# Second attention of a convolution sequence: the first projection's products ordered by input half, and the second item's denominators issued behind their step's filler

## The chip, the cores and the metric

The kernel runs on one core of a Trainium2 chip, in one launch, in float32 throughout. The metric is the device time of one execution in microseconds (us); lower is better. Times given for a kernel are medians of several runs.

## The reference

The input x has 16 images of 256 channels and 32x32 positions (1024 positions each). Two layers are applied to every image on its own. Cut to what matters here:

```python
# layer 0: attention with 4 heads of 64, softmax over the keys, a projection and a residual
qkv = xs @ w_proj + b_proj ; attn = softmax(q k^T * 64**-0.5) ; x = attn v @ w_out + b_out + xs
# layer 1, first half: group norm, attention with 8 heads of 32, a projection and a residual
qkv = group_norm(x) @ qkv_w.T
attn = softmax(q k^T * 32**-0.5 + phys_bias)
x = x + (attn v) @ proj_w.T + proj_b
# layer 1, second half: group norm and a two-layer MLP with GELU and a residual
x = x + mlp_w2 gelu(mlp_w1 group_norm(x) + mlp_b1) + mlp_b2
```

The change lies in layer 1's attention, called the second attention below (keys and tiles ending in `_b` or `b_...`); layer 0's is the first (`_a`).

## The kernel before, in words

**Stages.** `first_pass` walks over the 16 images (batches 0 to 15). For each it runs the first attention of image b, then dense work (the MLP's hidden layer of image b-1 and the products q, k, v of both attentions), then the second attention of image b. Work that does not depend on the attention is placed inside the second attention's steps as *filler*: the MLP's second layer of image b-1 (`reduce`, tiles m, products numbered 1 to 7) and products of the next image (v_a). Batches 1 to 14 take one form (`by_fold`); batches 0 and 15 take another, in which denominators are made in another way.

**Items and steps of the second attention.** An image has 1024 queries (two halves t of 512) and 8 heads (two halves c of 4 heads). An item is one pair (t, c): item 0 is (0,0), item 1 is (0,1), items 2 and 3 are the second query half. Each item goes over the 1024 keys in four units of two key blocks. `attention_b` is a generator: step n issues the scores of unit n (`scores`, tiles s_b, L569), weighs the unit before it (`weigh`, tiles acc_b, L621), and issues the additions of the exponentials on VectorE (tiles es_b, L595). The exponentials are ScalarE's (e_b, L582). Items 0 to 3 have units 0-3, 4-7, 8-11, 12-15.

**The planner.** `run` drives the generator. After step n it calls `later.tick()`, which runs what has come due, and then the filler listed for that step (`fill[n]`). `later.after(k, f)` puts f off by k ticks. All engines execute their own instructions in the order issued, so a place in this list is a place in each queue.

**Denominators.** When item i's last unit is weighed, `fold` packs its 128x2048 sums (es_b) into two slots of a tile `packed` of four slots (item 0 and 2: slots 0 and 1; item 1 and 3: slots 2 and 3). It uses one DMA from SyncE's queue and an accumulating one from GpSimd's queue (L651, L652). Some ticks later `normalise_folded` runs:

1. 8 matmuls on TensorE reduce `packed` to den (128x128) in PSUM bank 1 (den_b, L661; the profile counts 16, two for each).
2. ScalarE copies den to SBUF (rd_b, L376), and SyncE's queue spreads it (sp_b, L381).
3. At the next tick VectorE takes the reciprocal (inv_b, L387).
4. SyncE's queue writes it to DRAM (row_b, four issues, L391) and broadcasts it back (rd_b<-row_b, four issues, L403).
5. Some ticks later VectorE multiplies the item's result by it (`scale`, L703).

PSUM bank 1 has a single buffer. The scores of each step write their second 512-column group to that bank too.

**The first projection.** When item 1 has been scaled, the projection of the first query half is due one tick later (`out_proj`, tiles j, L357): two output halves co, each the sum over two input halves kc, each in four column strips of 32, so 16 matmuls (32 in the profile). Input half kc=0 is item 0's result, kc=1 is item 1's. Inside the second attention the two output halves share one two-bank PSUM tile, and both are read out after all products (ScalarE, L747). The readout goes to a *home*: slots 2 and 3 of the packed tile, handed over in `spare["home"]`. The projection of the second half is issued later, inside the next image's first attention.

**Who else uses the home.** While it is set, products 6 and 7 of the MLP are copied by ScalarE (L1213) into slot `number - 4` of the packed tile, that is slots 2 and 3. VectorE adds them to x from there (L1234).

**The step of the change.** Item 1 is folded in step 8, and its denominators come due at the tick of step 10. The filler of step 10 is product 6 in two parts of 256 columns (m, two times 32 matmuls in the profile). So TensorE's order in step 10 before the change is: weighing, den_b of item 1, product 6, then step 11's scores.

Of the kernel before, what the change touches and what calls it, by code (L numbers as in the profile page):

```python
# [14 lines left out]
P = 128  # L15
# [244 lines left out]
def first_pass(ctx, tc, x, out, k):  # L260
    nc = tc.nc
    B, C, S = x.shape
    CC, SB, NT = C // P, S // P, S // TB
    HC = k["m1b"].shape[1]
    later = Later()
# [44 lines left out]
    def wide(name, n=None):  # L310
        if n is None:
            n = next(m for m in order if m not in kept)
        use(n)
        return ps_s.tile([P, 2, TB], F32, tag=f"s{n}", name=name)

    def bank(name, n):
        return ps_a.tile([P, TB], F32, tag=f"b{n}", name=name)
# [36 lines left out]
    def product(o, w, r, **flags):  # L354
        for c0 in range(0, P, cols[0]):
            sl = slice(c0, c0 + cols[0])
            nc.tensor.matmul(o[sl], w[:, sl], r, **flags)  # L357
# [12 lines left out]
    def weights_tile(name):  # L370
        return work.tile([P, 4, TB], F32, tag="e", name=name, bufs=4)

    spread_out, spare = {}, {}

    def denominators(key, den, d, full, waits, then, parts=1):
        nc.scalar.copy(d, den)  # L376
# [165 lines left out]
    def attention_b(b, qT, kT, v, project):  # L542
# [9 lines left out]
        res, sums, packs, parts, count = {}, {}, [], [], [0]  # L552
# [94 lines left out]
        def fold(i, r):  # L647
            if i == 0:
                packs.append(act.tile([P, 4, TB], F32, tag="res", name=f"packed_{key}"))
            packed = packs[0][:, i % 2 * 2 : i % 2 * 2 + 2]  # L650
            nc.sync.dma_start(packed, sums[i][:HALF])  # L651
            nc.gpsimd.dma_start(packed, sums[i][HALF:], accum_op=ALU.add)  # L652
            later.after(3 if i == 1 else 4, lambda: normalise_folded(i, r, packed))

        def normalise_folded(i, r, packed):
            c = items[i][1]
            q = TB // G
            den = bank(f"den_{key}_{i}", 1)[:, :q]
            for m in range(2):
                for n in range(G):  # L660
                    nc.tensor.matmul(  # L661
                        den[n * D : (n + 1) * D, :], k["folded"][:, c, m],
                        packed[:, m, n * q : (n + 1) * q], start=m == 0, stop=m == 1,
                    )
            if i == 1:
                spare["home"] = packs[0]
            full = work.tile([P, TB], F32, tag="full", name=f"rd_{key}_{i}", bufs=2)
            denominators(
                f"{key}_{i}", den, full[:, :q], full, (1, 2 if i < 2 else 4),
                lambda full: scale(i, r, False, full), G,  # L670
            )
# [29 lines left out]
        def scale(i, r, last, full):  # L701
            t, c = items[i]
            tc.keep_in_program_order(nc.vector.tensor_mul(r, r, full))  # L703
            if c == CC - 1:
                issue = project(t, res[t])
                if last and b + 1 < B:
                    handed.append(issue)
                else:
                    later.after(1, issue)
# [23 lines left out]
    def out_proj(key, w, src, bias, xs, t, stats, then):  # L733
        todo = list(range(CC))

        def issue(cos=range(CC), apart=False):
            home = None if apart else spare.pop("home", None)
            apart = apart or cols[0] == P
            if not apart:
                both = wide(f"{key}_{t}")  # L740
            ps = {}

            def leave(co):
                y = xs[:, co, t * TB : (t + 1) * TB]
                if home is not None:
                    held = home[:, 2 + co]
                    nc.scalar.activation(  # L747
                        held, ps[co], AF.Identity, bias=bias[:, co : co + 1]
                    )
                    later.after(1, lambda: add_up(co, y, held))  # L750
                    return
                else:
                    nc.vector.scalar_tensor_tensor(
                        y, ps[co], bias[:, co : co + 1], y, ALU.add, ALU.add
                    )
                nc.vector.bn_stats(stats[:, co, t, :], y)
                todo.remove(co)

            def add_up(co, y, held):
                with tc.issue_after(spread_out["es"].ins):  # L760
                    nc.vector.tensor_add(y, y, held)
                    nc.vector.bn_stats(stats[:, co, t, :], y)

            for co in cos:
                ps[co] = bank(f"{key}_{t}_{co}", co) if apart else both[:, co, :]
                for kc in range(CC):
                    product(
                        ps[co],
                        w[:, kc, co * P : (co + 1) * P],
                        src(kc),  # L770
                        start=(kc == 0),
                        stop=(kc == CC - 1),
                    )
                if apart:
                    leave(co)
            if not apart:
                for co in cos:
                    leave(co)
            if not todo and then:
                then()  # L780

        return issue
# [310 lines left out]
    def mlp(b, xb):  # L1093
# [93 lines left out]
        def reduce(number, right, outs, then, part=0, parts=1):  # L1187
            size = TB // parts
            at = slice(part * size, (part + 1) * size)
            ps = wide(f"m2_{b}_{number}_{part}")[:, 0, :size]  # L1190
            for i in range(n4):
                product(
                    ps, blocks[2][number - 1][:, i * P : (i + 1) * P], gs[(*right, i)][:, at],
                    start=(i == 0), stop=(i == n4 - 1),
                )
            bias, num, m = None, 1, None
            if len(outs) == 1:
                bias = k["m2b2"]

                num = 2 if b == B - 1 and number == 7 else 1  # L1200
            elif number in (2, 5):
                bias = k["m2b"]
            co = outs[0][0]
            if len(outs) == 2 or "home" in spare:

                if not lent:
                    lent.append(act.tile([P, 4, TB], F32, tag="v0", name=f"lent_{b}"))
                if len(outs) == 2:
                    m = lent[0][:, number % 4]
                else:  # L1210
                    m = spare["home"][:, number - 4]
                if bias is not None:
                    nc.scalar.activation(m[:, at], ps, AF.Identity, bias=bias[:, co : co + 1])  # L1213
                    bias = None
                else:
                    nc.scalar.copy(m[:, at], ps)
                if part < parts - 1:
                    return
                ps = m
            assert parts == 1 or m is not None  # L1220

            def add_up():
                for co, t, plus in outs:
                    missing[co, t] -= 1
                    n = TB // num
                    for u in range(num):
                        sl = slice(t * TB + u * n, t * TB + (u + 1) * n)
                        y, p = xb[:, co, sl], ps[:, u * n : (u + 1) * n]
                        if bias is not None:
                            nc.vector.scalar_tensor_tensor(  # L1230
                                y, p, bias[:, co : co + 1], y, ALU.add, ALU.add
                            )
                        else:
                            (nc.vector.tensor_add if plus else nc.vector.tensor_sub)(y, y, p)  # L1234
                        if not missing[co, t]:
                            nc.sync.dma_start(out[b, co * P : (co + 1) * P, sl], y)
                if then:
                    for i in range(n4) if b == B - 1 else (None,):
                        combine(*then, True, i)


            if len(outs) == 2 and b < B - 1:
                later.after(1, add_up)
            else:
                add_up()
# [7 lines left out]
    def run(stage, fill=None):  # L1253
        for n, _ in enumerate(stage):
            pieces = fill.get(n, ()) if fill else ()
            if n > last:
                run_pieces(pieces, False)
            later.tick()
            if n <= last:
                run_pieces(pieces, False)  # L1260

    def run_pieces(pieces, tick=True):
        for piece in pieces:
            piece()
            if tick:
                later.tick()
# [14 lines left out]
    ps, n = bank("bqk", 0), brow.shape[0]  # L1281
# [4 lines left out]
    start = first_qk[::2] + first_qk[1::2] + first_v  # L1286
# [441 lines left out]
```

## Time and profile before

| | |
|---|---|
| median of 3 runs | 3623.34 us (3620.74 to 3624.38) |
| the profiled execution's own time | 3623.73 us |
| its span | 3621.7 us, at a granted TensorE clock of 0.998 |
| TensorE matmul busy | 3588.2 us (99%), 35,565 matmuls |
| VectorE busy | 2781.4 us (77%) |
| ScalarE busy | 2283.7 us (63%) |
| GpSimd busy | 229.9 us (6%) |

The profile is of one execution. The times are those of whole executions, 2.0 us longer than the span in the profiled one. The page of the profile gives busy time by engine, a chain of work that ended last, and groups of instructions by line and tile. The trace behind it gives each instruction's start. Ends of matmuls are modelled, so idle time of TensorE that is shorter than the modelled tail of a matmul does not show as idle. It shows as a longer distance from one start to the next.

### The profile page before, as it was taken

How to read it: one execution, taken by the hardware profiler on the slowest of the kernel's cores; microseconds unless marked ns; L12 is line 12 of the kernel's file. 1: busy time of each engine (PE TensorE's matmuls, PEld its weight loads, DVE VectorE, ACT ScalarE, POOL GpSimd, SP SyncE). 2: the span in 40 equal slices, each digit the busy share in tenths (PEclk: the TensorE clock that was granted, in tenths of full speed). 3: DMA queues.
4: the chain of work that ended last, by engine and by line, in shares of the span. 5: the costliest groups of instructions: out<-in, count | busy, mean ns of one | idle time of the engine just before them, and what ended most of it. 6: DMA issues, size and time to landing. Idle time of an engine off the chain costs nothing.

```text
span 3621.7 us, 81706 instructions
## 1 busy us (share of the span) xinstructions
PE 3588.2 (99%) x35565; PEld 1471.2 (41%) x35565; DVE 2781.4 (77%) x3181; ACT 2283.7 (63%) x3197; POOL 229.9 (6%) x317
## 2 busy tenths in 40 slices
PE   9999999999999999999999999999999999999998
PEld 3434344443443434434344443434434444343433
DVE  5586887868878687876878878688786977868887
ACT  4565757657576674756758566575765757657572
POOL 4000100001000010000000001000010100001000
PEclk9999999999999999999999999999999999999999
DMA  3011221203112131221312213121121212213100
GB/s 129 10 49 39 58 76 37 78 28 68 68 37 75 37 83 45 44 68 39 81 45 52 66 33 81 45 55 63 38 76 45 55 62 48 72 39 65 59 23 23
DMA packets 81572, 198.30 MB, mean 55 GB/s; under 512 B 37974, under 2 KB 38742, under 8 KB 75062
## 3 DMA queue, kind: packets, MB, share of 16 engines
q1 hardware_dynamic: 71828, 164.39, 14.9%
q0 software_dynamic: 7632, 28.21, 5.1%
q8 instruction: 281, 4.60, 0.5%
q14 instruction: 85, 0.70, 0.1%
q10 hardware_dynamic: 1746, 0.40, 0.1%
HBM read 125.85 MB, written 22.27 MB: 41 GB/s over the span
## 4 chain that ended last, share of the span: by engine, by line
PE 81%; DVE 8%; issue 4%; DMA 3%; SPq 2%; ACT 1%; DVEq 0%; ACTq 0%; POOL 0%
PE s_a L428 12%; PE acc_a L451 12%; PE m L1105 10%; PE s_b L569 8%; PE acc_b L621 8%; PE m L357 7%; DVE es_b L595 4%; PE qk_b L1011 3%; PE qk_a L1011 3%; PE v_b L357 3%; PE o L357 3%; PE j L357 3%; PE v_a L357 2%; DMA rd_b<-row_b 2%; PE qk7y_b L1011 1%
## 5 line engine op out<-in xcount | busy, mean ns | idle before, releaser
L582 ACT ACTIVATE e_b<-s_b 128x1024 f32<-128x1024 f32 (+1 forms) x1280 | 982.0, 865 | 137.1 <-PE s_b L569 137.1
L595 DVE TENSOR_TENSOR es_b<-es_b,e_b 128x2048 f32<-128x2048 f32 (+1 forms) x460 | 881.7, 1935 | 101.9 <-ACT e_b L582 85.9
L438 ACT ACTIVATE e_a<-s_a 128x1024 f32<-128x1024 f32 x512 | 520.8, 1024 | 360.2 <-PE s_a L428 357.4
L428 PE MATMUL s_a<-q,k 64*64 64x512 f32 x4096 | 544.3, 593 | 0.0
L451 PE MATMUL acc_a<-e_a,v 64*64 64x512 f32 x4096 | 540.2, 589 | 0.0
L569 PE MATMUL s_b<-q,k 32*64 32x512 f32 x8192 | 527.4, 600 | 4.0 <-DVE res_b L639 2.0
L465 DVE TENSOR_TENSOR es_a<-es_a,e_a 128x1024 f32<-128x1024 f32 x384 | 474.1, 1235 | 69.2 <-ACT e_a L438 49.7
L621 PE MATMUL acc_b<-e_b,v 128*32 128x512 f32 x4096 | 492.1, 598 | 0.0
L357 PE MATMUL m<-g,w 128*32 128x256 f32 (+1 forms) x6456 | 416.6, 385 | 0.0
L357 PEld LDWEIGHTS m<-g,w 128*32 128x32 f32 x6456 | 223.9, 111 | 204.3 <-issue 58.9
L451 PEld LDWEIGHTS acc_a<-e_a,v 64*64 64x64 f32 x4096 | 188.0, 133 | 251.5 <-issue 215.1
L569 PEld LDWEIGHTS s_b<-q,k 32*64 32x64 f32 x8192 | 175.8, 130 | 257.5 <-issue 132.6
L428 PEld LDWEIGHTS s_a<-q,k 64*64 64x64 f32 x4096 | 175.9, 133 | 246.7 <-issue 209.5
L621 PEld LDWEIGHTS acc_b<-e_b,v 128*32 128x32 f32 x4096 | 108.4, 109 | 351.6 <-ACT e_b L582 194.7
L1105 PE MATMUL m<-gn_h,w 128*128 128x512 f32 x512 | 242.3, 601 | 2.9 <-DVE x L1230 1.3
L595 DVE TENSOR_TENSOR es_b<-e_b,e_b 128x2048 f32<-128x2048 f32 (+1 forms) x72 | 147.0, 2051 | 127.8 <-ACT e_b L582 127.8
L1169 DVE TENSOR_TENSOR g<-g,g 128x512 f32<-128x512 f32 (+1 forms) x185 | 195.7, 1069 | 1.2 <-PE m L357 0.8
L1105 PE MATMUL m<-hs,w 128*128 128x512 f32 x384 | 177.9, 592 | 0.1
L1120 ACT ACTIVATE g<-g,m1b 128x512 f32<-128x512 f32 x128 | 91.7, 720 | 110.9 <-DVE g L1149 83.3
L1105 PEld LDWEIGHTS m<-gn_h,w 128*128 128x128 f32 x512 | 93.2, 190 | 118.6 <-issue 100.5
L1120 ACT ACTIVATE g<-m,m1b 128x512 f32<-128x512 f32 x128 | 80.9, 683 | 76.6 <-PE m L1105 76.6
L357 PE MATMUL v_a<-wp,x 128*32 128x256 f32 (+1 forms) x1856 | 121.5, 379 | 0.0
(215 smaller groups left out, 3537.5 us busy)
## 6 DMA issues: line engine op xcount, KB each, us to landing
w<-w_kept SPq DMA_DIRECT2D x30, 1792.0 KB
packed_b<-es_b SPq DMA_DIRECT2D x42, 512.0 KB
packed_b<-es_b POOLq DMA_DIRECT2D x42, 512.0 KB, 6.2
d_a<-row_a SPq DMA_DIRECT2D x64, 256.0 KB
rd_b<-row_b SPq DMA_DIRECT2D x252, 64.0 KB
out_dram<-x SPq DMA_DIRECT2D x63, 256.0 KB
x<-in_x_dram SPq DMA_DIRECT2D x30, 512.0 KB
qk<-qk_kept SPq DMA_DIRECT2D x14, 1024.0 KB
```

The lines of the kernel that those rows point to most:

```text
L357: nc.tensor.matmul(o[sl], w[:, sl], r, **flags)
L428: nc.tensor.matmul(s[h : h + HALF, g, :], kT[g * D : (g + 1) * D, c, kb * P + h : kb * P + h + HALF], qT[g * D : (g + 1) * D, c, t * TB : ...
L438: nc.scalar.activation(e, s, AF.Exp, scale=float(D) ** -0.5)
L451: nc.tensor.matmul(accs[i][h][g * D : (g + 1) * D, :], v[h * HALF : (h + 1) * HALF, kb, c * 2 + g], e[h * HALF : (h + 1) * HALF, g, :], st ...
L465: nc.vector.tensor_add(sums[i], held[i] if kb == 1 else sums[i], e)
L569: nc.tensor.matmul(outs[g][h : h + HALF, :], kT[g * D : (g + 1) * D, c, k0 : k0 + HALF], qT[g * D : (g + 1) * D, c, t * TB : (t + 1) * TB] ...
L582: nc.scalar.activation(to, s, AF.Exp, scale=float(D) ** -0.5)
L595: ins = nc.vector.tensor_add(d, (d if kb else es[0][:, g : g + step]), es[m][:, g : g + step])
L621: nc.tensor.matmul(acc[g * D : (g + 1) * D, :], v[:, kb + m, c * G + g], es[m][:, g, :], start=(m == 0), stop=(m == 1),)
L1011: nc.tensor.matmul(to, w, x[right], start=first, stop=True, skip_group_check=not first)
L1105: nc.tensor.matmul(ps, blocks[1][number - 1][:, i * P : (i + 1) * P], inputs[b][number], start=first, stop=True, skip_group_check=not first,)
L1169: (nc.vector.tensor_add if plus else nc.vector.tensor_sub)(d, d, more)
```

## The change

There are two edits to the order of issue, and one of a buffer that goes with the second.

1. In `out_proj`, where the two output halves share a tile, all products of input half 0 are issued first (both output halves), then all of input half 1. Before, output half 0 was finished before output half 1 was begun. Where the halves have banks of their own the order stays.
2. The denominators of item 1 (batches 1 to 14) are put on a list `behind` when they come due, and `run` issues them after the step's filler instead of ahead of it. The tick on which the rest depends stays the same.
3. Product 6 goes to slot 0 of the packed tile in place of slot 2 (`number % 6 * 3`; product 7 keeps slot 3), and `spare["home"]` is set when item 1 is folded.

```diff
-    spread_out, spare = {}, {}
+    spread_out, spare, behind = {}, {}, []
...
-            later.after(3 if i == 1 else 4, lambda: normalise_folded(i, r, packed))
+            if i == 1:
+                spare["home"] = packs[0]
+                later.after(3, lambda: behind.append(lambda: normalise_folded(i, r, packed)))
+            else:
+                later.after(4, lambda: normalise_folded(i, r, packed))
...
-            if i == 1:
-                spare["home"] = packs[0]
...
+            def part(co, kc):
+                product(
+                    ps[co],
+                    w[:, kc, co * P : (co + 1) * P],
+                    src(kc),
+                    start=(kc == 0),
+                    stop=(kc == CC - 1),
+                )
+
             for co in cos:
                 ps[co] = bank(f"{key}_{t}_{co}", co) if apart else both[:, co, :]
+            if apart:
+                for co in cos:
+                    for kc in range(CC):
+                        part(co, kc)
+                    leave(co)
+            else:
                 for kc in range(CC):
-                    product(
-                        ps[co],
-                        w[:, kc, co * P : (co + 1) * P],
-                        src(kc),
-                        start=(kc == 0),
-                        stop=(kc == CC - 1),
-                    )
-                if apart:
-                    leave(co)
-            if not apart:
+                    for co in cos:
+                        part(co, kc)
                 for co in cos:
                     leave(co)
...
-                    m = spare["home"][:, number - 4]
+                    m = spare["home"][:, number % 6 * 3]
...
             if n <= last:
                 run_pieces(pieces, False)
+            while behind:
+                behind.pop(0)()
```

No instruction is added or removed. On VectorE's, GpSimd's and SyncE's queues none changes its place. On TensorE's and ScalarE's queues the denominators of item 1 (8 matmuls and one copy) move behind product 6 (32 matmuls and two copies) in 14 batches, and the projection's products change order in all 16.

## Prediction

> **What bounds the kernel now.** I read the page first, then the waits of the projection's tile j, then the timeline at the two places that the change touches. Of the page, busy times and the chain that ended last:
>
> ```profile
> PE 3588.2 (99%) x35565; PEld 1471.2 (41%) x35565; DVE 2781.4 (77%) x3181; ACT 2283.7 (63%) x3197; POOL 229.9 (6%) x317
> ...
> PE 81%; DVE 8%; issue 4%; DMA 3%; SPq 2%; ACT 1%; DVEq 0%; ACTq 0%; POOL 0%
> ```
>
> TensorE sets the time almost everywhere. As no matmul is added or removed, the change can only shift stalls. The chain leaves TensorE once in each second attention and comes back at the projection. Timeline of TensorE there, batch 1 (start, length, engine, line, tiles, count, idle before and what ended it):
>
> ```profile
> 428.31 1.04 PE L357 MATMUL j<-res_b,wpj 128*32 128x512 f32 x8
> 430.72 2.78 PE L357 MATMUL j<-res_b,wpj 128*32 128x512 f32 x24 [1.37 <-DVE res_b L703]
> ```
>
> The 8 matmuls are output half 0 with input half 0. Then TensorE waits for VectorE's scaling of item 1. Undisturbed, a group of four 512-column matmuls starts every 0.42 us; here 1.96 us pass, so the stall is S = 1.54. The timeline gives the same distance for batches 1 to 14: 1.96, 1.07, 1.62, 1.15, 1.11, 0.94, 0.90, 0.51, 2.20, 1.06, 1.17, 0.94, 1.30, 0.50. Less 0.42 each, the stalls sum to 10.6 us. In batches 0 and 15 the projection has no such gap. So 10.6 us, 0.29% of the time, is all that edit 1 can touch.
>
> What makes the scaling late is not TensorE. The reciprocal of item 1 starts at 417.18 and the scaling at 429.97; between them lie SyncE's four row issues, the write, four broadcast issues and their landing. From item 0's scaling to item 1's reciprocal VectorE has no gap, and the distance is 6.39 to 6.43 us in every batch in which I read it, also in three in which TensorE had just lost a microsecond. VectorE and the transfers run on their own clock here, and TensorE waits for it.
>
> The second place, step 10 of batch 1:
>
> ```profile
> 402.48 0.62 PE L661 MATMUL den_b<-packed_b,folded 128*32 128x128 f32 x16
> 402.91 3.64 PE L357 MATMUL m<-g,w 128*32 128x256 f32 x64
> 404.10 0.34 ACT L376 COPY rd_b<-den_b 128x128 f32<-128x128 f32 x1
> 406.12 0.61 SPq L381 DMA_DIRECT2D sp_b<-rd_b  x1
> 406.48 1.97 PE L569 MATMUL s_b<-q,k 32*64 32x512 f32 x32
> 406.62 0.47 ACT L1213 ACTIVATE packed_b<-m,m2b 128x256 f32<-128x256 f32 x1 [1.20 <-PE m L357]
> ```
>
> Denominators, filler, next scores. ScalarE has emptied PSUM bank 1 at 404.44, two microseconds before the scores need it. In batches 2, 8 and 14 the denominators' packed transfer is late (batch 2):
>
> ```profile
> 624.73 1.47 PE L621 MATMUL acc_b<-e_b,v 128*32 128x512 f32 x12
> 627.00 0.64 PE L661 MATMUL den_b<-packed_b,folded 128*32 128x128 f32 x16 [0.81 <-DMA packed_b<-es_b]
> ```
>
> From the last weighing group to den_b it is 0.43 us in 11 batches, and 1.42, 1.35 and 1.41 in these three: stalls of 0.99, 0.92 and 0.98.
>
> **The Trainium skill.** "PSUM — Partial Sum Buffer", section "Engine vs sequencer instructions": ScalarE and VectorE work strictly first in, first out, and matmuls start and complete in program order. The trace agrees: TensorE stood 1.37 us at j with ready scores behind it. The same page, "PSUM bank collisions raise a hardware error": two engines may not touch one bank and quadrant at once, so the guard is by bank. The trace shows that guard as a wait (batch 0, below). "Perfetto Trace Analysis", section "Tensor Engine Instruction (MATMUL, LD_WEIGHTS)": a matmul's end is estimated. The trace agrees (0.81 us shown idle at 627.00, 0.99 from starts), so I use starts.
>
> **The change part by part.**
>
> *Edit 1.* Same 32 recorded matmuls. With both output halves of input half 0 first, 16 of them (four groups) need no scaling of item 1; before, 8. Two more groups, 2 x 0.42 = 0.85 us, move under the stall. Alone it gains min(0.85, S) per batch: 8.6 us over the 14. The readout is unchanged: ScalarE's first copy (L747, 433.57) starts after the last matmul, not after output half 0.
>
> *Edit 2, what it removes.* The three late transfers get 3.45 us more (64 matmuls of product 6, 402.91 to 406.36), against a lateness of 1 us. TensorE then reaches the projection 0.99, 0.92 and 0.98 us sooner. This is no gain of its own, as it only lengthens S there; with it, S' = 1.64, 1.01 and 1.06 in batches 2, 8 and 14.
>
> *Edit 2, what it adds.* den_b now ends just before step 11's scores, whose second group writes bank 1. Working for batch 1: product 6 starts at 402.48, den_b at 405.93, its last matmul at 406.28. ScalarE's copy starts 0.33 us after the last den_b start (batch 2: 627.38 to 627.71) and lasts 0.27 to 0.34, so it ends at 406.88 to 406.95; the wait ends 0.05 later. The second product 6 copy is ahead of it in ScalarE's queue, ready at 406.18 and 0.47 long, so it doesn't hold it up. Without the wait the scores would start at 406.48. So TensorE loses d = 0.45 to 0.52, taken as 0.47, in each of 14 batches. The trace has this sequence in batch 0, where no filler stands between (TensorE, then ScalarE):
>
> ```profile
> 178.22 1.04 PE L678 MATMUL den_b<-es_b,eones 128*32 128x512 f32 x8
> 179.21 2.81 PE L569 MATMUL s_b<-q,k 32*64 32x512 f32 x32
> ...
> 179.38 0.63 ACT L376 COPY rd_b<-den_b 128x512 f32<-128x512 f32 x1
> ```
>
> The scores span 2.81 us against 1.97: 0.85 lost, with a copy of 512 columns and ScalarE busier. That is the upper end of d; the lower is 0 (a wait can't give time back). Queued behind the waiting scores are their weighing and ScalarE's exponentials, for which VectorE waits: the first tile is ready at 409.60 and VectorE takes it at 411.99, so 0.47 is covered, with 1.9 us left.
>
> *Edit 2, the inversion.* ScalarE's copy ends about 2.5 us later (406.9 for 404.4). SyncE's spread is issued at about 407.1 for 406.12, as SyncE was busy till then; it landed by 410.2, so by about 411.2. VectorE takes the reciprocal at 417.18. Cost nothing; cover 6 us, and 7.0 to 9 us before the change in all 14 batches. SyncE's next issue waits for VectorE until 412.09.
>
> *Edit 3.* Product 6 in slot 0 no longer overwrites what den_b still has to read; slot 0 was last read by item 0's den_b, 17 us earlier. Item 2's packing into slot 0 must wait for VectorE's addition of product 6 (ends 412.06), but is issued at 416.73 anyway. Nothing, with 4.7 us of cover. Product 6's copies come 0.43 us sooner, unused.
>
> *Sum.* TensorE reaches the projection d later, less the stall removed; the scaling is where it was. Gain per batch = min(0.85, S' - d). With d = 0.47 the 14 batches give 0.85, 0.85, 0.73, 0.26, 0.22, 0.05, 0.01, 0.54, 0.85, 0.17, 0.28, 0.05, 0.41, 0.59: **5.9 us**. In batches 0 and 15 edit 1 gains nothing. TensorE keeps this: VectorE is idle for 0.46 us before 460.17, waiting for ScalarE, so it has caught up, and the second half's projection at 464.99 needs a scaling that ended at 457.25. Against the profiled execution's 3623.73 that is 3617.8; that execution stands 0.4 above the median, so I give 3617.4.
>
> **The rivals.**
>
> *The wait at bank 1 is covered* (d near 0, for instance because the first score group fills it). For it: two groups of scores don't use bank 1. Against: batch 0 lost the full time. Gain 10.3 us: 3613.
>
> *The wait costs more than it hides: slower.* Place: the second score group of step 11. Break-even is d = 0.96, the mean of S'; at d = 1.5 the loss is 7.6 us: 3631. This needs ScalarE to reach den_b's copy a microsecond late, behind both product 6 copies (2 x 0.47) and a first exponential. Against: the first product 6 copy starts at 404.94, long before.
>
> *The time is given back.* If VectorE, not sped up, held TensorE later in the batch, 3623.3 would stay. Against: the idle VectorE at 460. A d of 0.85 has the same answer (gain 1.5).
>
> **How the numbers follow.** A measurement of this kernel tells about 0.2%, 7.2 us, from no change. The main case, d of 0.3 to 0.65, gains 3.9 to 7.7 us: 0.62. Covered wait, 8 to 12 us: 0.20. Given back or d near 0.85: 0.12. Slower: 0.06. About a quarter of the main case, by the spread of the stalls between executions, passes 7.2 us: faster 0.20 + 0.18 = 0.38, slower 0.06, same 0.56. Range 3611.0 to 3623.9: from most of the covered case to time given back.
>
> **What would show it.** Right: j as 16 and 16 matmuls, the stall between them shorter by about 0.85 less what TensorE arrives late or early; den_b without a wait for a packed transfer in any batch; the scores of step 11 spanning about 2.4 us, waiting for ScalarE's L376. Wrong: scores of 1.97 us there (covered), scaling more than 0.3 us later after item 0's (the inversion moved), or j undelayed and the batch no shorter (given back).

## The result, and the profile after

| | before | after |
|---|---|---|
| median | 3623.02 us (22 runs, 3618.81 to 3625.18) | 3617.38 us (22 runs, 3614.09 to 3619.0) |
| ratio, 95% interval | | 0.9985 [0.9979, 0.9991] |
| profiled execution, its span | 3623.73, 3621.7 us | 3614.09, 3612.0 us |

The kernel is 5.6 us faster, 0.16%. The interval lies clear of no change (it allows a gain of 3.3 to 7.6 us). The gain is below the 0.2%, 7.2 us, that the prediction took as the least that a measurement can tell from no change; 22 runs a side tell less than that. The profiled execution of after is the fastest of its 22, so the two spans differ by more than the medians do. That excess is accounted for below.

The page of after, busy times and the chain that ended last:

```profile
PE 3590.2 (99%) x35565; PEld 1471.8 (41%) x35565; DVE 2780.2 (77%) x3181; ACT 2284.7 (63%) x3197; POOL 227.4 (6%) x317
...
PE 91%; DVE 4%; issue 2%; DMA 2%; SPq 1%; ACT 1%; ACTq 0%; DVEq 0%; POOL 0%
```

The work is the same, 35,565 matmuls in both. TensorE's share of the chain rose from 81% to 91% and VectorE's halved. The starts below say why: in half of the batches TensorE no longer has to wait for VectorE at the projection. Timeline of TensorE there, batches 1, 2 and 8 of after:

```profile
424.83 3.91 PE L357 MATMUL j<-res_b,wpj 128*32 128x512 f32 x32
```
```profile
647.52 3.62 PE L357 MATMUL j<-res_b,wpj 128*32 128x512 f32 x32
```
```profile
1982.27 1.90 PE L357 MATMUL j<-res_b,wpj 128*32 128x512 f32 x16
1984.62 1.92 PE L357 MATMUL j<-res_b,wpj 128*32 128x512 f32 x16 [0.46 <-DVE res_b L705]
```

Where the scaling is still late, the 32 matmuls now break into 16 and 16, not 8 and 24. Batch 2 shows an undisturbed projection: 3.62 us. Batch 1 takes 3.91; 0.26 of the difference lies between its 16th and 17th start, too little to show as idle. By starts, the stall at the projection (S in the prediction) is zero in 7 of the 14 batches and 0.26, 0.18, 0.10, 0.63, 0.19, 0.28 and 0.85 in batches 1, 6, 7, 8, 12, 13 and 14: 2.5 us in all, against 10.6 before.

Steps 10 and 11 of batch 1 in after, TensorE with its weight loads (PEld), ScalarE and SyncE's queue in one timeline (other engines and some weight loads left out):

```profile
401.14 1.05 PE L357 MATMUL m<-g,w 128*32 128x256 f32 x16
402.00 0.62 PE L665 MATMUL den_b<-packed_b,folded 128*32 128x128 f32 x16
402.25 0.47 ACT L1222 ACTIVATE packed_b<-m,m2b 128x256 f32<-128x256 f32 x1 [1.20 <-PE m L357]
402.55 2.42 PE L569 MATMUL s_b<-q,k 32*64 32x512 f32 x32
402.69 0.27 ACT L376 COPY rd_b<-den_b 128x128 f32<-128x128 f32 x1
403.00 0.22 PEld L569 LDWEIGHTS s_b<-q,k 32*64 32x64 f32 x14 [0.26 <-ACT rd_b L376]
403.02 0.61 SPq L381 DMA_DIRECT2D sp_b<-rd_b  x1
404.90 0.64 PE L621 MATMUL acc_b<-e_b,v 128*32 128x512 f32 x4
```

Filler, denominators, scores. ScalarE reads den from 402.69 to 402.96, and the weight load of the second score group stands until then. So the scores last 2.42 us by the modelled end. From the first score to the first weighing it is 2.35 us (402.55 to 404.90), against 1.90 before. The scores lose 0.45 us, the prediction's d: **d = 0.45 us, in each of the 14 batches**.

The answers of the trace for the tile den_b. Columns: what ended the wait, us in all, times. Two lines of before:

```profile
  DMA packed_b<-es_b: 2.3, 3
...
  PEld s_b L569: 7.9, 18
```

The same answer in after:

```profile
its engine sat idle before it (us, times) until:
  issue: 15.0, 50
  PE den_b L680: 9.1, 15
  ACT e_b L582: 5.7, 19
  DVE es_b L595: 0.5, 2
who waited for it (us, times):
...
  PEld s_b L569: 11.6, 32
```

No wait for a packed transfer is left. There were three before, and den_b now stands 0.20 us behind the last filler matmul in all 14 batches. The scores, in turn, wait for den_b 32 times, where before it was 18: one new wait in each of the 14 batches. This answer gives idle time of the weight loads, not what TensorE lost: 3.7 us more here, against 6.3 by starts (run 3 below has as many waits and no loss).

**The sum of the two executions.** After's span is 9.7 us shorter.

| term, by starts, 14 batches together | us |
|---|---|
| the projection, first to last start: 53.4 to 45.1 | -8.3 |
| den_b's waits for packed transfers: 2.9 to 0 | -2.9 |
| step 11's scores: 1.90 to 2.35 each | +6.3 |
| two gaps elsewhere, batch 7 before and batch 13 after | -0.7 |
| before the first second attention, which the change does not touch | -3.9 |
| sum | -9.5 |

The 3.9 us lies at the start of the program: the products v_a of the first image begin at 28.29 us before and at 24.38 after. The granted clock of the first 30 us was 0.89 in that execution of before and 1.00 in that of after. Without it the two profiles differ by 5.8 us, near the 5.6 of the medians. Of these 5.8, the three terms that the change acts on give 4.9. Another 0.7 is the difference of the two gaps, which lie in the dense work, outside the second attention, and 0.2 stands in no term.

### The profile page after: what moved, and what is told of

Its sections match the earlier page's. It is cut to its first block, busy times and chain, and to the rows that moved or that the text cites. A ratio compares the mean times of both kernels' runs of the same rounds, so it can differ in the third digit from the quotient of the medians.

```text
span 3612.0 us, 81707 instructions
## 1 busy us (share of the span) xinstructions
PE 3590.2 (99%) x35565; PEld 1471.8 (41%) x35565; DVE 2780.2 (77%) x3181; ACT 2284.7 (63%) x3197; POOL 227.4 (6%) x317
## 4 chain that ended last, share of the span: by engine, by line
PE 91%; DVE 4%; issue 2%; DMA 2%; SPq 1%; ACT 1%; ACTq 0%; DVEq 0%; POOL 0%
PE s_a L428 12%; PE acc_a L451 12%; PE s_b L569 12%; PE acc_b L621 11%; PE m L1114 10%; PE m L357 9%; PE qk_b L1020 3%; PE qk_a L1020 3%; PE v_b L357 3%; PE o L357 3%; PE j L357 3%; PE v_a L357 3%; DVE es_b L595 2%; PE qk7y_b L1020 1%; PE qk7y_a L1020 1%
```

## The experiments

Four kernels ran beside one set of runs of the kernel before (median 3622.69 us, 29 runs). The last two ran beside another (3622.22, 9 runs).

**1. The order alone.** Of the change, only the hunk of `out_proj`.

```diff
+                for kc in range(CC):
+                    for co in cos:
+                        part(co, kc)
```

> Edit 1 alone (products of the first projection by input half; the denominators of item 1 stay ahead of the filler). Theory (per batch TensorE gains the smaller of 0.85 us and the stall at the projection, and the denominators behind the filler cost 0.45 us of the changed kernel's gain): 8.6 us off the kernel before, about 3614.5, which is 3 us less than the whole change; the scores of step 11 span 1.90 us as before, the stall between the 16th and 17th projection matmul is what was left of it before less 0.85, and now and then item 1's denominators wait up to 1 us for their packed transfer. Rival (the late denominators are what pays, the order of products only moves the wait): little or no gain, 3621 to 3623.

Measured: 3613.68 us (7 runs), ratio 0.9974 [0.9962, 0.9985], so 9.0 us faster. Projection of batch 1:

```profile
427.95 1.90 PE L357 MATMUL j<-res_b,wpj 128*32 128x512 f32 x16
430.30 1.92 PE L357 MATMUL j<-res_b,wpj 128*32 128x512 f32 x16 [0.46 <-DVE res_b L703]
```

The stall is 0.63 there and 2.2 us over all batches. Step 11's scores last 1.90 everywhere, and den_b is late in four batches (0.37, 1.06, 0.34, 0.92). Edit 1 alone brings more than the whole change: six of its seven runs are faster than the fastest of the change's 22.

**2. Denominators behind the filler, with product 6's new slot.** Edits 2 and 3: all of the change but that hunk.

```diff
+            if i == 1:
+                spare["home"] = packs[0]
+                later.after(3, lambda: behind.append(lambda: normalise_folded(i, r, packed)))
...
+                    m = spare["home"][:, number % 6 * 3]
...
+            while behind:
+                behind.pop(0)()
```

> Edits 2 and 3 alone (denominators of item 1 behind the filler, product 6 in slot 0; products of the projection in the old order). Theory: the scores of step 11 span 2.35 us, TensorE comes to the projection 0.45 us later (0.5 us sooner where the packed transfer was late) and its stall there is shorter or longer by just that, since the scaling's time is fixed by VectorE and the transfers: no change, 3623.0 within 1.5 us. Rival (the move is the part that pays): 3618 or less. Rival (the wait at bank 1 is on the path): 6 us slower, 3629.

Measured: 3625.16 us (13 runs), ratio 1.0007 [0.9999, 1.0015]: 2.5 us slower, with an interval that just includes no change. It lies outside the 3623.0 within 1.5 us that was expected, and fits neither rival. The scores of step 11 take 2.35 us in all batches and no packed transfer is late. The stall stays after the 8th matmul:

```profile
429.87 2.78 PE L357 MATMUL j<-res_b,wpj 128*32 128x512 f32 x24 [0.80 <-DVE res_b L705]
```

Its sum is 9.9 us. TensorE loses d = 0.45 us a batch and arrives later at a scaling that is where it was, so by the prediction's model nothing should be lost: the stall should have fallen by what the scores lose. The scaling was not quite where it was: after item 0's it came on average 0.20 us later than before, 2.8 us over 14 batches, which is the size of the miss. Why it came later is open (below).

**3. The whole change, the wait at bank 1 taken out.** Item 1's den goes to a tile of the two-bank pool. The scores of step 11 use that tile too, but they write it last, where bank 1 comes second.

```diff
-            den = bank(f"den_{key}_{i}", 1)[:, :q]
+            name = f"den_{key}_{i}"
+            den = (wide(name)[:, 0, :] if i == 1 else bank(name, 1))[:, :q]
```

> The whole change, with item 1's denominators accumulated in a tile of the score pool instead of bank 1, the one that is written last in step 11. Theory (the 0.45 us is the guard of bank 1): scores of step 11 back to 1.90 us, in all 14 batches; gain min(0.85, stall plus late transfer), 10.3 us off the kernel before, about 3612.7, 5 us less than the change. Rival (the time is ScalarE's queue or the switch from the denominators' matmuls to the scores, whatever the bank): scores stay at 2.3 us and 3617.

Measured: 3611.54 us (7 runs), ratio 0.997 [0.9958, 0.9981]: 11.2 us faster than before and 5.8 faster than the whole change, by the medians. Batch 1, TensorE, then ScalarE and a weight load of the scores:

```profile
403.95 0.62 PE L666 MATMUL den_b<-packed_b,folded 128*32 128x128 f32 x16
404.50 1.97 PE L569 MATMUL s_b<-q,k 32*64 32x512 f32 x32
...
404.63 0.27 ACT L376 COPY rd_b<-den_b 128x128 f32<-128x128 f32 x1
404.98 0.18 PEld L569 LDWEIGHTS s_b<-q,k 32*64 32x64 f32 x8 [0.25 <-ACT rd_b L376]
```

The copy stands where it stood, 0.68 us after den_b's start, and the scores run through in 1.97 (1.90 by starts, in all 14 batches). The scores still wait for ScalarE's copy, 32 times and 11.4 us in the answer for den_b, but with a weight load at 404.98, when the copy has just ended (404.90), and they lose nothing. So d is not the cost of the late copy as such, nor of the step from den's matmuls to the scores: it is paid because the scores need the bank early. 14 x 0.45 = 6.3 us is nearly the whole difference to the change, and the stalls at the projection take back a little (4.0 us against 2.5), as TensorE arrives earlier. All seven runs are faster than the fastest of the change's 22.

**4. The whole change, the bank held longer.** Three more copies of den on ScalarE, into parts of rd_b that are overwritten later.

```diff
+            if i == 1:
+                for n in range(1, G):
+                    nc.scalar.copy(full[:, n * q : (n + 1) * q], den)
```

> The whole change, and ScalarE reads item 1's denominators three more times (copies of 128 columns into the part of the tile that the broadcast overwrites later), so that bank 1 is held longer. Theory: each copy adds some 0.25 us, the scores of step 11 span about 3.1 us (d about 1.2), and by min(0.85, S' - d) the gain turns into a loss of about 3 us: 3626, 8 to 9 us more than the change. Rival (TensorE's lateness there is given back before the next image, since VectorE sets the pace): 3617 to 3619.

Measured: 3621.28 us (13 runs), ratio 0.9996 [0.9987, 1.0004]: 3.9 us slower than the whole change by the medians, 1.4 faster than before (an interval that includes no change). Batch 1, copies and scores:

```profile
405.87 2.92 PE L569 MATMUL s_b<-q,k 32*64 32x512 f32 x32
...
406.00 0.27 ACT L376 COPY rd_b<-den_b 128x128 f32<-128x128 f32 x1
406.16 0.61 ACT L676 COPY rd_b<-den_b 128x128 f32<-128x128 f32 x3
406.83 0.24 PEld L569 LDWEIGHTS s_b<-q,k 32*64 32x64 f32 x16 [0.77 <-ACT rd_b L676]
```

The expected 3626 was missed, because the dose was mis-sized: the three copies overlap and hold the bank some 0.5 us longer, not 0.75. d came out at 0.96 by starts, the break-even of the prediction, and the kernel came out within 0.04% of before. With d = 0 (run 3), 0.45 (the change) and 0.96 (this run), the model's gains of 10.3, 6.1 and 0.0 us stand against 11.2, 5.6 and 1.4 measured, in the same order and each within 1.4.

**5. The kernel before, its projection one step later.** Nothing of the change. The projection is issued a step later in batches 1 to 14, and the filler of step 15 goes to step 14 in its place.

```diff
-                    later.after(1, issue)
+                    later.after(2 if by_fold else 1, issue)
...
-                [], first[2:3],
+                first[2:3], [],
```

> The kernel before with the first projection issued one step later (step 15) and step 15's filler (products of the next image) moved to step 14 in its place; products in the old order, denominators ahead of the filler. Theory (TensorE's stall at the projection is nothing but waiting for a scaling with its own clock): no gap inside the projection in any batch, all 10.6 us of it gained, 3612 or less; as the scores that follow the projection no longer follow it directly, the 0.6 us that they wait there for its readout may go as well, down to 3604. The late packed transfers (1 us in some batches) stay. Rival (the wait moves to another place, since VectorE's additions for the projection now come behind the last exponentials): 3618 to 3623.

Measured: 3603.36 us (5 runs), ratio 0.9944 [0.993, 0.9957]: 18.9 us faster. Batch 1, TensorE, and VectorE's scaling:

```profile
429.86 1.98 PE L569 MATMUL s_b<-q,k 32*64 32x512 f32 x32
...
433.94 2.33 PE L357 MATMUL j<-res_b,wpj 128*32 128x512 f32 x20
...
429.58 0.69 DVE L703 TENSOR_TENSOR res_b<-res_b,rd_b 128x512 f32<-128x512 f32 x1 [2.85 <-DMA rd_b<-row_b]
```

The scaling ends 3.7 us before the projection starts (3.7 to 5.2 in the 14 batches), and no batch has a gap inside the projection: that is the 10.6 us of S. The rest lies in a wait that the prediction did not name. In before and after alike, the answer for the tile j has among those who waited for it:

```profile
  PEld s_b L569: 5.5, 14
```

These are the scores that follow the projection, waiting for ScalarE's readout of its two-bank tile. Batch 1 of after, TensorE, then its weight loads:

```profile
428.67 2.54 PE L569 MATMUL s_b<-q,k 32*64 32x512 f32 x32
...
430.12 0.21 PEld L569 LDWEIGHTS s_b<-q,k 32*64 32x64 f32 x8 [0.39 <-ACT packed_b L749]
```

They take 2.54 us, against 1.98 where nothing stops them. In run 5 those scores come first, and the row is gone from the answer. From one projection to the next, batches without a stall are 0.56 us shorter (221.96 in run 1, 221.40 here), so 14 x 0.56 = 7.8. Together 18.4, against 18.9 measured.

**6. Runs 3 and 5 together, with both edits of the order.** The whole change, den in the two-bank pool, and the projection a step later.

> The whole change with item 1's denominators in a tile of the score pool, and the first projection one step later as in e4_late. Theory: neither the packed transfer nor bank 1 nor the scaling makes TensorE wait; against e4_late it gains only the late transfers, some 3 us: 3601 to 3609. Rival: no more than the kernel with the tile of the score pool alone, 3611.5, as something else takes the stall's place.

Measured: 3600.48 us (5 runs), ratio 0.9939 [0.9926, 0.9953]: **21.7 us faster than before, some 16 faster than the change** (21.7 less 5.6), the best of the kernels and just under the range expected. Batch 1:

```profile
404.90 0.62 PE L666 MATMUL den_b<-packed_b,folded 128*32 128x128 f32 x16
405.45 1.97 PE L569 MATMUL s_b<-q,k 32*64 32x512 f32 x32
...
433.21 3.62 PE L357 MATMUL j<-res_b,wpj 128*32 128x512 f32 x32
```

Scores of 1.97 behind den_b, and an unbroken projection. The 2.9 us over run 5 are near the late packed transfers of run 5's own profile (2.2 us, in batches 6, 8 and 14) and what was expected, some 3 us. The intervals of runs 5 and 6 overlap, so this last step is the least certain.

## Why the prediction was right

Predicted 3617.4 us, a gain of 5.9 us on the profiled execution; measured 3617.38, a gain of 5.6. That the medians agree to 0.02 us is luck, since the runs of one kernel spread over 5 us; so is a part of the agreement in gain, because the terms of the change sum to 4.9 us in the two traces, 1.0 less than predicted. The mechanism is what the runs support. Step by step:

- **TensorE sets the time, and S is all that edit 1 can touch.** Right. S fell from 10.6 to 2.5 us. The reciprocal of item 1 still comes 6.39 to 6.43 us after item 0's scaling in every batch and in every one of the kernels: VectorE keeps its own pace, as read. The new wait of the scores didn't reach it, so the cover named for VectorE's first tile held.
- **Edit 1 hides 0.85 us per batch, 8.6 alone.** Right: 9.0 (run 1), as 16 and 16 matmuls.
- **Late packed transfers vanish.** Right: no wait is left in any batch. Batches 8 and 14 are late in all three kernels that leave the denominators ahead of the filler; the others vary (2 before; 6 and 12 in run 1; 6 in run 5). The sum is 2.9, 2.7 and 2.2 us.
- **d = 0.47, of 0.45 to 0.52.** Right: 0.45, in all 14 batches. The range of the main case began at 0.3. Runs 3 and 4 show that the bank's handover to ScalarE costs it.
- **The inversion costs nothing.** Mostly right: ScalarE's copy ends at 402.96, the spread is issued at 403.02 and has landed by 406.22, where GpSimd's addition of it starts; the reciprocal follows at 413.25. Those 7 us are the cover. Yet in after's execution the scaling of item 1 came on average 0.24 us later after item 0's than in before's (18.86 against 18.62 us). As the reciprocal did not move, the excess lies between reciprocal and scaling, and there in the broadcasts: the first is issued on average 5.37 us after the reciprocal in before and 5.38 in after, and from its issue to the scaling it is 6.85 and 7.08. An excess of that size would account for the 2.5 us of stall that are left where the model leaves 1.0 (S' less d less 0.85 where that is positive: 0.22, 0.32 and 0.46 in batches 1, 2 and 9). This is the term of the sum that was mis-sized, by 1.5 us; a d that is 0.02 us smaller gives 0.3 of it back. The excess was 0.20 in run 2, 0.13 in run 4, 0.03 in run 3 and -0.04 in run 6, which all have the inversion, and -0.04 in run 1 and -0.10 in run 5, which have not. It falls in different batches each time, and the inversion alone doesn't bring it, as run 6 shows. Whether the change has a part in it stays open.
- **Edit 3 costs nothing.** It was not run by itself. The sum above leaves 0.2 us for it and for all else.

The rivals. *The wait is covered*: refuted, since the scores span 2.35 us in every batch, and shown as a kernel of its own in run 3, where the forecast for it (3613) was 1.5 us too high. *The wait costs more than it hides*: did not happen. Run 4 brought d to the break-even, and the time came to within 1.4 us of before, so the point is where it was put; beyond it nothing was run. *The time is given back*: refuted. From the last start of batch 14's first projection to the end of the program it is 289.4 us in both traces, and runs 3 and 5 pass on larger gains.

Where the forecast was too narrow: it looked for gains only inside the projection. The wait of the next scores for its readout, 5.5 us in the answer for the tile j, lay beside it and was not priced. With it gone and the projection later, run 5 gained 18.9 us with neither edit of the change.

## What to carry to other kernels

Read each part of a change against the same stall. Here the reorder was worth 9.0 us alone; the companion move removed 2.9 us of waits and added 14 waits of 0.45 us on one PSUM bank, so that the two together were worth 5.6. A denser order inside a stall hides part of it; issuing the waiting work where its input is long ready removes all of it, and here also a second wait behind it. When matmuls move directly ahead of others that write the same bank, count the handover to the engine that reads it, or give the result a bank that they write later (run 3).

## What the runs showed of the hardware

- The handover of a PSUM bank, in run 3's and after's timelines: ScalarE's copy of 128 columns starts 0.69 us after den_b's first matmul (402.00 to 402.69), lasts 0.27, and the next matmul's weight load into that bank's group starts 0.04 us later.
- Small ScalarE copies overlap: one of 128 columns took 0.27 us, three in a row 0.61, and each further one delayed the bank's release by about 0.17 us.
- From item 1's reciprocal to its scaling, with four row writes and four broadcasts of 64 KB between them, it took 11.6 to 13.4 us over all kernels, and within one execution it differed from batch to batch by over a microsecond (11.7 to 13.4 in after). SyncE's queue takes 3.9 us for the four writes and 4.2 for the four broadcasts in batch 1.
